# A bidirectional state-space mixer on one core: the logarithm of the step sizes behind the gates, three taps ahead of the states

## The chip, the core and the metric

The kernel runs on one core of a Trainium2 chip. The core has a matrix engine (PE, with its weight loads shown apart as PEld), a vector engine (DVE), an activation engine (ACT), a general-purpose engine (POOL) and a queue processor (SP), which issues most of the transfers here. The engines run their own instruction streams in order and wait for each other by semaphores. The metric is the device time of one execution in microseconds, the median of several runs.

## What is computed

An input of 8 batches x 1024 tokens x 128 channels passes three blocks: attention (L0), a mixer that scans the tokens in both directions (L1_attn), and a filter bank (L1_ffn). The change lies in the mixer and in the last part of the attention, where the mixer's first step sizes are made. For each direction the mixer computes

```python
zxbcdt = x @ in_proj
z, xbc, dt = jnp.split(zxbcdt, [D_INNER, D_INNER + CONV_DIM], axis=-1)
xp = jnp.pad(xbc, ((0, 0), (K - 1, 0), (0, 0)))
conv = sum((xp[:, i:i + l, :] * conv_w[:, i] for i in range(K))) + conv_b
xbc = jax.nn.silu(conv)
xh, Bm, Cm = jnp.split(xbc, [D_INNER, D_INNER + D_STATE], axis=-1)
dt = jax.nn.softplus(dt + dt_bias)
A = -jnp.exp(A_log)
y = _ssd(xh, dt, A, Bm, Cm) + xh * D[None, None, :, None]
yg = y.reshape(b, l, D_INNER) * jax.nn.silu(z)
yn = yg * jax.lax.rsqrt(jnp.mean(yg * yg, -1, keepdims=True) + EPS) * norm_w
return yn @ out_proj
```

K is 4. The second direction does the same on the reversed tokens with other weights. `_ssd` cuts the tokens into chunks of 64: within a chunk a decay-weighted product of C, B and x, between chunks a state that is passed on with a decay. The two parts that the change moves are one tap of `conv` and the logarithm in `softplus`.

## The kernel before

The mixer (from about 450 to 1010 us of the span) handles 16 units, each a batch b and a direction d, in the order (0,0), (0,1), (1,0) and so on. The order of the instructions on every engine is written out by hand (`manual_schedule`): they run in the order in which the Python code issues them. One pass of the loop `for at, u in enumerate(units[:-1])` (line 1285 on) works on three units: it finishes `last`, carries u through its states and outputs, and prepares `following`. Where u is of the first direction and a batch b + 1 is left (b = 0 to 6), the pass also turns that batch's tokens and makes its step sizes for both directions (`fresh`).

What the prediction needs of a pass, in order of issue:

- `going = steps(...)`, a generator, makes the step sizes. Softplus is max(v, 0) + log(1 + exp(-|v|)) with a correction: v and -|v| on DVE (`sp_v`, `sp_e`), the exponential on ACT (line 509), 1 + e on DVE (`sp_u`, line 512), the logarithm on ACT (`sp_l`, line 514), and the rest (`dt`, `da`, lines 516 to 521) on DVE. The code between two `yield`s is issued at one `next(going)`.
- `end(last, ...)` projects `last` (PE, `spo`), and `scale_rows(last)` scales the rows on ACT (eight activations, line 1216). A `next(going)` follows, which holds lines 512 and 514.
- `weigh_decays(u, 1)` and `convolve(following, 0, ...)` on DVE: the convolution of channels 0 to 127 of `following`. The tap with the bias is on ACT (`first_tap`, line 972), the three others are DVE instructions of 128x1024 (line 980). Two of them are issued here.
- `project_z` and `activate_z` for two halves: PE computes `pz`, ACT makes the gates `zs` by Silu (line 993). Then `first_tap(following, 1)`.
- `from_row(following, ...)` on POOL (line 924) starts the decays `lm` of `following`. A dependence added by hand puts it behind `following.convolved`, the last tap issued by then, where u is of the first direction. `between(following, AF.Relu, 1.0)` on ACT (line 934) follows it.
- `chunk_states(u)` on PE (`pst`, line 1082), `pass_states(u)` on DVE (lines 1096 and 1099), with four transfers `moved` out of `state` that SP issues (line 1112), two at the middle and two at the end.
- `next(going)`: lines 516 to 521.
- The third tap, then `activate_x(following, 0)` on ACT (Silu, line 985), `project_bc` on PE (`pb`, 16 matmuls, line 1002), `activate_bc` on ACT (`bt`, `ct`, line 1018), three taps for the other 128 channels, `outputs(u, 0)` on PE (`sy`), `add_decays` (`pdec`, copied out as `cums` and `dsum`), `activate_x(following, 1)`, `outputs(u, 1)`, `add_rows(last)`.
- The next pass begins with `turn_decays` (`cs`), `take_decays` and `turn_x` (`sx` on PE, which reads both `xs`; `xdt` on DVE).

PSUM buffers of the pool `ps_w` are two and taken in turn: `pb` takes the one that the first `pz` had, so it waits for the first gate. `pst` takes those of `spo` and `misc` in the pool `ps_s`.

ACT holds one set of function tables at a time. The exponential, the logarithm and Silu are in three different sets here, and an `ACT_TABLE_LOAD` stands in the stream ahead of each activation whose function the active set lacks.

In the attention, whose loop counts slots n, the step sizes of batch 0 are made at slots 117 (three parts), 121 (lines 512 and 514) and 123 (the rest).

Of the kernel before, what the change touches and what calls it, by code (L numbers as in the profile page):

```python
# [45 lines left out]
def fast_kernel(ctx: ExitStack, tc: tile.TileContext, a: dict, out: bass.AP, bad: bass.AP):  # L46
# [420 lines left out]
    pad = KC - 1  # L467
# [12 lines left out]
    def steps(b, seq, pd):  # L480

        xt = seq["xt"]

        def small(tag):
            return tokens.tile([P, NT, n2], F32, tag=tag, name=f"{tag}{b}")

        def wide(t):  # L490
            return t.rearrange("p d h -> p (d h)").unsqueeze(1).to_broadcast([P, NT, n2])

        pd = pd[:, : NT * n2].rearrange("p (j h) -> p j h", j=NT)
        for j in range(NT):
            nc.tensor.matmul(
                pd[:, j, :],
                lhsT=xt[:, pad + j * P : pad + (j + 1) * P],
                rhs=wdt.rearrange("p d h -> p (d h)"),
                start=True,
                stop=True,  # L500
            )
        yield
        v = small("sp_v")
        nc.vector.tensor_tensor(v, pd, wide(dtb), ALU.add)
        e = small("sp_e")
        nc.vector.tensor_scalar(e, v, -1.0, None, ALU.mult)
        nc.vector.tensor_tensor(e, e, v, ALU.min)
        yield
        nc.scalar.activation(e, e, AF.Exp)
        yield  # L510
        u = small("sp_u")
        nc.vector.tensor_scalar(u, e, 1.0, None, ALU.add)
        lg = small("sp_l")
        nc.scalar.activation(lg, u, AF.Ln)
        yield
        nc.vector.scalar_tensor_tensor(u, u, -1.0, e, ALU.add, ALU.subtract)
        nc.vector.tensor_tensor(lg, lg, u, ALU.subtract)
        dt = small("dt")
        nc.vector.scalar_tensor_tensor(dt, v, 0.0, lg, ALU.max, ALU.add)
        da = tokens.tile([P, 2, NH, NT], F32, tag="da", name=f"da{b}")  # L520
        nc.vector.tensor_tensor(
            da.rearrange("p d h j -> p j d h"),
            dt.rearrange("p j (d h) -> p j d h", d=2),
            nega.unsqueeze(1).to_broadcast([P, NT, 2, NH]),
            ALU.mult,
        )
        seq["dt"], seq["da"] = dt, da
# [63 lines left out]
    with ExitStack() as s:  # L591
# [179 lines left out]
        going, making, coming = transform_taps(p1, ps_t, tables), transforms(p1, tables), qkv(0)  # L771
# [14 lines left out]
        for n in range(len(units) + 2):  # L786
            if n < len(units):
                prs[n] = scores(*units[n])
            if 2 <= n and units[n - 2][2] % 2:
                b, half, j = units[n - 2]  # L790
                total(b, half)
                if j == NT - 1:
                    ending = weighted(b, half, avs[half], sums["d"])
            if 1 <= n < len(units) + 1:
                b, half, j = units[n - 1]
                weigh(b, half, j, prs.pop(n - 1))
                if j == NT - 1:
                    nc.vector.tensor_copy(avs[half], sums["o"])
            if n % 8 in (0, 1, 3, 5, 7):
                next(ending, None)  # L800

            if n % 16 == 14 and n // 16 + 2 < B:
                coming = qkv(n // 16 + 2)
            if n % 16 in (14, 15, 1, 3, 5, 6, 7, 10, 11, 12, 13):
                next(coming, None)
            if n % 16 in (4, 6, 8, 12, 14):
                next(mixing, None)
            if n >= 16 * (B - 1):
                next(going, None)
            if n in (9, 25, 41, 57, 73):  # L810
                next(making, None)

            if n in (99, 115):
                norm = normalize(bridge, n // 112)
            elif n in (103, 119):
                norming = normalized(n // 112, bridge, *norm)
                next(norming)
            elif n in (105, 122):
                next(norming, None)
            elif n == 113:  # L820
                turn_tokens(0, seqs[0], ps_t.tile([P, T], F32, tag="t", name="px0"))
            elif n == 117:
                sizes = steps(0, seqs[0], ps_t.tile([P, T], F32, tag="t", name="pd0"))
                for _ in range(3):
                    next(sizes)
            elif n in (121, 123):
                next(sizes, None)
        assert not [*mixing, *making, *going, *coming]

# [8 lines left out]
    with ExitStack() as s:  # L838
# [46 lines left out]
        def turn_decays(u):  # L885

            nc.tensor.transpose(u.pcs, u.cums[:, 0], ident[: NT * NH, : NT * NH])
            u.cs = p2.tile([P, NH, NT], F32, tag="cs", name=f"cs{u.tag}")
            nc.scalar.copy(u.cs, u.pcs.rearrange("p (h j) -> p h j", h=NH))
# [80 lines left out]
        def first_tap(u, n):  # L970
            xp, body = u.xp[n]
            nc.scalar.activation(
                u.xs[:, n, :], xp[:, body], AF.Identity, bias=cb[u.d][:, n, :], scale=cw[u.d][:, n, pad : pad + 1]
            )

        def convolve(u, n, taps=range(pad)):
            acc, xp = u.xs[:, n, :], u.xp[n][0]
            for i in taps:
                at = i if u.d == 0 else pad - i
                u.convolved = nc.vector.scalar_tensor_tensor(  # L980
                    acc, xp[:, at : at + T], cw[u.d][:, n, i : i + 1], acc, ALU.mult, ALU.add
                )
# [294 lines left out]
        for at, u in enumerate(units[:-1]):  # L1277
            following = units[at + 1]
            after_it = units[at + 2] if at + 2 < len(units) else None

            fresh = u.b + 1 if u.d == 0 and u.b + 1 < B else 0
            turn_decays(following)
            if at == 0:
                between(u, AF.Relu, 1.0)
            take_decays(following)
            between(u, AF.Exp, -1.0, (0,))
            turn_x(u)
            weigh_start(u, u.convolved)
            if last:
                add_x(last)  # L1290
            turn_b(u)
            if fresh:
                turn_tokens(fresh, seqs[fresh], wide_psum(ps_w, f"px{fresh}"))
            between(u, AF.Exp, -1.0, (1,))
            project_x(following, 0)
            copy_x(following, 0)
            if last:
                gate(last, 0)
                gate(last, 1)
            project_x(following, 1)  # L1300
            copy_x(following, 1)
            causal(u)
            decayed_x(u)
            weigh_decays(u, 0)
            going = iter(())
            if fresh:
                going = steps(fresh, seqs[fresh], wide_psum(ps_w, f"pd{fresh}"))
            if last:
                end(last, ps_s, (lambda: next(going)) if fresh else None)
            elif fresh:  # L1310
                next(going)
            next(going, None)
            next(going, None)
            first_tap(following, 0)
            if last:
                scale_rows(last)
            next(going, None)

            b = (u.b + 2) % B
            norm = None  # L1320
            if u.d == 1 or u.b == B - 1:
                norm = normalize(bridge, b)
            weigh_decays(u, 1)
            convolve(following, 0, range(pad - 1))
            for n in range(2):
                project_z(u, n)
                activate_z(u, n)
            first_tap(following, 1)
            for _ in normalized(b, bridge, *norm) if u.d else ():
                pass  # L1330
            from_row(following, shifted[-1] if u.d else following.convolved)
            between(following, AF.Relu, 1.0)
            chunk_states(u)
            pass_states(u)
            next(going, None)
            if stored:
                reload(stored)
            stored = None
            convolve(following, 0, range(pad - 1, pad))
            activate_x(following, 0)  # L1340
            project_bc(following)
            activate_bc(following)
            convolve(following, 1)
            outputs(u, 0)
            if after_it:
                add_decays(after_it)
            activate_x(following, 1)
            outputs(u, 1)
            if last:
                add_rows(last)  # L1350
                stored = last if last.d else None
            last = u

        u = units[-1]
# [1104 lines left out]
```

## Time and profile before

| what | us |
|---|---|
| median of 3 runs (lowest, highest) | 1420.11 (1420.01, 1421.38) |
| the profiled execution | 1414.25 |
| its span | 1412.4 |
| PE busy in the span | 1325.0 |
| DVE busy | 1093.9 |
| ACT busy | 916.0 |
| POOL busy | 530.2 |
| one table load on ACT | 1.28 |
| logarithms, in the whole kernel | 8, of 0.26 each |
| DVE taps (line 980), in the whole kernel | 96, 121.7 in total |

The profile is of one execution, which here was 5.9 us shorter than the median of the runs. A timeline line gives the start, the length, the engine, the line of the kernel, the operation, the tile written and the tiles read, the shapes and how many instructions are merged; in brackets stands how long the engine was idle before, and whom it waited for. `x28` with 5.46 us is 28 instructions that took 5.46 us together. A line of the waits gives the total in us, how often, and the longest. "issue" is idle time for which the profile shows no cause. `PEld` is the weight load of a matmul.

### The profile page before, as it was taken

The page shows a single profiled execution, that of the slowest core. Times are in us where ns is not written, and L with a number is a line of the kernel's source. Part 1 is how long each engine was busy: PE and PEld are TensorE (multiplying, and loading weights), DVE is VectorE, ACT ScalarE, POOL GpSimd, SP SyncE. Part 2 cuts the span into 40 slices and gives each one's busy share as a digit, 9 for nine tenths or more (in the row PEclk, how much of TensorE's full clock was granted, in tenths as well). Part 3 has the DMA queues.
Part 4 walks back from the last instruction along what each step waited for, and adds up shares of the span by engine and source line. Part 5 has one row for each costly group of instructions (what it writes and reads, how often), then busy time and mean ns, then how long its engine had stood idle before and what let it go on. Part 6 is the DMA issues. An engine that isn't in the chain of part 4 may idle for free. (4 is left out here: it accounts for less than half of the span.)

```text
span 1412.4 us, 45313 instructions
## 1 busy us (share of the span) xinstructions
PE 1325.0 (94%) x19798; PEld 836.2 (59%) x19798; DVE 1093.9 (77%) x2141; ACT 916.0 (65%) x1423; POOL 530.2 (38%) x510
## 2 busy tenths in 40 slices
PE   5999999999999899999999999998799899999977
PEld 2323333233333466666666666665689899999964
DVE  6789888787768698978897988889644677777745
ACT  3766666766757777878787878786454555555530
POOL 2426865875610333425243434343476111111100
PEclk9999999999999999999999999999999999999999
DMA  7101111110000543434344445441459233222257
GB/s 179 46 1 31 46 38 38 38 50 27 8 1 2 124 86 77 107 77 106 82 102 91 104 92 114 89 110 42 135 189 233 76 86 81 72 78 71 71 186 299
DMA packets 139382, 123.09 MB, mean 87 GB/s; under 512 B 44808, under 2 KB 118152, under 8 KB 135080
## 3 DMA queue, kind: packets, MB, share of 16 engines
q1 hardware_dynamic: 137048, 115.93, 32.1%
q10 hardware_dynamic: 2128, 4.19, 0.8%
q8 instruction: 157, 2.57, 0.8%
q14 instruction: 49, 0.40, 0.1%
HBM read 78.15 MB, written 34.08 MB: 79 GB/s over the span
## 5 line engine op out<-in xcount | busy, mean ns | idle before, releaser
L707 ACT ACTIVATE pr<-pt 128x1024 f32<-128x1024 f32 x256 | 248.1, 1021 | 114.9 <-PE pt L702 113.5
L732 DVE TENSOR_TENSOR two<-pr,pr 128x1024 f32<-128x1024 f32 x128 | 162.3, 1308 | 19.2 <-ACT pr L707 18.7
L1525 ACT COPY gs<-pg 128x512 f32<-128x512 f32 x256 | 132.4, 603 | 64.1 <-PE pg L1512 48.3
L1523 DVE COPY gs<-pg 128x512 f32<-128x512 f32 x256 | 158.7, 683 | 14.7 <-PE pg L1512 9.7
L702 PE MATMUL pt<-q,k 32*128 32x512 f32 x1024 | 157.6, 648 | 9.4 <-ACT pr L707 4.7
L1512 PE MATMUL pg<-taps,mst 32*128 32x128 f32 x4096 | 145.6, 281 | 4.2 <-ACT gs L1525 3.4
L1512 PEld LDWEIGHTS pg<-taps,mst 32*128 32x128 f32 x4096 | 133.8, 190 | 16.2 <-issue 11.4
L723 PE MATMUL po<-pr,v 128*32 128x512 f32 x1024 | 139.7, 603 | 0.0
L938 POOL TENSOR_TENSOR ec<-ec,ct 128x2048 f32<-128x2048 f32 x16 | 83.6, 5226 | 131.8 <-ACT cums L880 69.8
L1546 PE MATMUL py<-gs,u 128*32 128x128 f32 (+1 forms) x4096 | 128.5, 277 | 1.2 <-issue 1.2
L1002 PE MATMUL pb<-bxt,wbc 128*128 128x512 f32 x256 | 115.7, 605 | 11.0 <-ACT zs L993 11.0
L980 DVE SCALAR_TENSOR_TENSOR xs<-xp,cw,xs 128x1024 f32<-128x1024 f32 x96 | 121.7, 1281 | 1.7
L1546 PEld LDWEIGHTS py<-gs,u 128*32 128x32 f32 (+1 forms) x4096 | 112.4, 141 | 8.7 <-issue 1.5
L1535 POOL TENSOR_SCALAR u<-u 128x512 f32<-128x512 f32 x16 | 23.9, 1495 | 227.8 <-DMA u<-ud 114.0
L702 PEld LDWEIGHTS pt<-q,k 32*128 32x128 f32 x1024 | 46.6, 185 | 87.2 <-issue 33.1
L1002 PEld LDWEIGHTS pb<-bxt,wbc 128*128 128x128 f32 x256 | 47.7, 191 | 69.3 <-issue 54.9
L1099 DVE SCALAR_TENSOR_TENSOR state<-state,dec,pst 128x64 f32<-128x64 f32 x448 | 87.3, 274 | 1.5 <-DVE state L1096 0.5
L1208 POOL TENSOR_TENSOR rms<-rms_v,mhalf 128x8 f32<-128x8 f32 x16 | 27.1, 1696 | 159.7 <-DVE rms_v L1206 159.7
L723 PEld LDWEIGHTS po<-pr,v 128*32 128x32 f32 x1024 | 27.6, 110 | 88.3 <-issue 84.1
L924 POOL TENSOR_TENSOR lm<-cs,lm 128x2048 f32<-128x2048 f32 x16 | 57.9, 3620 | 46.9 <-DVE xs L980 31.4
L743 PE MATMUL pd<-two,ones 128*32 128x512 f32 x512 | 73.9, 612 | 0.2
L1178 PEld LDWEIGHTS spo<-wo,y 128*128 128x128 f32 x512 | 62.2, 192 | 15.3 <-issue 10.2
(288 smaller groups left out, 2757.7 us busy)
## 6 DMA issues: line engine op xcount, KB each, us to landing
lm<-cd SPq DMA_DIRECT2D x32, 512.0 KB
ec<-cd SPq DMA_DIRECT2D x32, 512.0 KB
ud<-sp SPq DMA_DIRECT2D x8, 1024.0 KB
u<-ud SPq DMA_DIRECT2D x32, 256.0 KB
yd<-sums SPq DMA_DIRECT2D x32, 256.0 KB
moved<-state SPq DMA_DIRECT2D x48, 128.0 KB
room<-yd SPq DMA_DIRECT2D x6, 1024.0 KB
X<-in_x SPq DMA_DIRECT2D x8, 512.0 KB
```

The costliest lines, as they stand in the source:

```text
L702: nc.tensor.matmul(pt[:, i, :], lhsT=k[rows, j * P : (j + 1) * P], rhs=q[rows, cols], start=True, stop=True)
L707: nc.scalar.activation(pr[:, 2 * g : 2 * g + 2, :].rearrange("p i t -> p (i t)"), pt.rearrange("p i t -> p (i t)"), AF.Exp, scale=SCALE,)
L723: nc.tensor.matmul(po[rows, :], lhsT=vs[b][:, j, rows], rhs=pr[:, h, :], start=(j == 0), stop=(j == NT - 1))
L732: nc.vector.tensor_tensor(two, sums["pr"][:, 2 * g : 2 * g + 2, :], pr[:, 2 * g : 2 * g + 2, :], ALU.add)
L938: t = nc.gpsimd.tensor_tensor(u.ec, u.ec, u.ct.unsqueeze(1).to_broadcast([P, NH, NT, L]), ALU.mult)
L980: u.convolved = nc.vector.scalar_tensor_tensor(acc, xp[:, at : at + T], cw[u.d][:, n, i : i + 1], acc, ALU.mult, ALU.add)
L1002: nc.tensor.matmul(u.pb[:, i * 512 : (i + 1) * 512], lhsT=wbc[u.d][:, k, :], rhs=xt[:, at : at + 512], start=(k == 0), stop=(k == KC - 1),)
L1099: nc.vector.scalar_tensor_tensor(u.state[:, k, h, :], u.state[:, k - 1, h, :], u.dec[:, c, h, j : j + 1], u.pst[c][:, j, h, :], ALU.mult, ...
L1512: nc.tensor.matmul(pts[g][:, e, :], lhsT=mst[rows, n * 4 + e, :], rhs=taps[rows, cols].rearrange("p f q m i -> p (f q m i)"), start=True, ...
L1523: nc.vector.tensor_copy(to, frm)
L1525: nc.scalar.copy(to, frm)
L1546: nc.tensor.matmul(py[t * 32 : t * 32 + 32 - 16 * m, q // 2, :], lhsT=u[:, i, m:, :, :, q * FC + f].rearrange("p k b i -> p (k b i)"), rhs ...
```

## The change

The logarithm gets a `yield` of its own ahead of it, so that 1 + e and the logarithm are issued at different places. In the mixer 1 + e stays behind `scale_rows`, and the logarithm is issued behind the gates and the first tap of the other channels, ahead of `from_row` and the Relu. In the attention 1 + e moves from slot 121 to slot 120, and the logarithm stays at 121.

In passes whose u is of the first direction (d = 0), all three DVE taps of channels 0 to 127 are issued ahead of the states (`pad - u.d` is 3), where two were. In the other passes (d = 1) it stays at two and one.

```diff
@@ -510,6 +510,7 @@
         yield
         u = small("sp_u")
         nc.vector.tensor_scalar(u, e, 1.0, None, ALU.add)
+        yield
         lg = small("sp_l")
         nc.scalar.activation(lg, u, AF.Ln)
         yield
@@ -823,7 +824,7 @@
                 sizes = steps(0, seqs[0], ps_t.tile([P, T], F32, tag="t", name="pd0"))
                 for _ in range(3):
                     next(sizes)
-            elif n in (121, 123):
+            elif n in (120, 121, 123):
                 next(sizes, None)
         assert not [*mixing, *making, *going, *coming]
 
@@ -1321,11 +1322,13 @@
             if u.d == 1 or u.b == B - 1:
                 norm = normalize(bridge, b)
             weigh_decays(u, 1)
-            convolve(following, 0, range(pad - 1))
+            soon = pad - u.d
+            convolve(following, 0, range(soon))
             for n in range(2):
                 project_z(u, n)
                 activate_z(u, n)
             first_tap(following, 1)
+            next(going, None)
             for _ in normalized(b, bridge, *norm) if u.d else ():
                 pass
             from_row(following, shifted[-1] if u.d else following.convolved)
@@ -1336,7 +1339,7 @@
             if stored:
                 reload(stored)
             stored = None
-            convolve(following, 0, range(pad - 1, pad))
+            convolve(following, 0, range(soon, pad))
             activate_x(following, 0)
             project_bc(following)
             activate_bc(following)
```

In the instruction streams of the changed kernel, the third tap also is the one that `from_row` waits for, and one table load more stands in each of the seven passes: the gates need Silu, the logarithm its own set, and `activate_x` Silu again.

## The prediction

> **What bounds the kernel now.** The page first: PE is busy for 94% of the span, but that is an average over stages. The chain that ended last reaches back only to 1014.58 us, behind the stage that is changed, so for the mixer I read waits and timelines. First the windows by stage and PE's list of waits, both for 480 to 945 us, the seven batches that loop through the mixer:
>
> ```profile
> 480.00:945.00 465.00, 442.58 (x6870) 301.59 (x6869) 395.95 (x867) 370.48 (x589) 172.55 (x95) 1.00 0.42 95
> PE pb L1002 <- ACT zs L993: 10.7, 14, 1.3
> PE sb L1048 <- DVE xdt L1034: 6.2, 14, 0.4
> PE sy L1147 <- issue: 3.5, 5, 0.8
> ```
>
> Columns of the first line: stretch, length, busy PE, PEld, DVE, ACT, POOL, clock, DMA share. PE is busy 442.6 of 465 us; the rest is nearly all in the next three lines (total, times, longest). PE is the bound, and its largest remaining hole is `pb` waiting for the gates `zs`. One pass of the loop in which it is long, u = (1, first direction), on ACT:
>
> ```profile
> 550.83 2.15 ACT L1216 ACTIVATE y<-spo,rms 128x128 f32<-128x128 f32 x8
> 553.00 1.28 ACT L514 ACT_TABLE_LOAD   x1
> 554.29 0.26 ACT L514 ACTIVATE sp_l<-sp_u 128x64 f32<-128x64 f32 x1
> 554.57 1.28 ACT L993 ACT_TABLE_LOAD   x1
> 555.86 1.94 ACT L993 ACTIVATE zs<-pz 128x1024 f32<-128x1024 f32 x2
> 557.69 1.24 ACT L972 ACTIVATE xs<-xp,cb,cw 128x1024 f32<-128x1024 f32 x1
> 558.82 2.00 ACT L934 ACTIVATE lm<-lm 128x1024 f32<-128x1024 f32 x2
> 563.77 1.06 ACT L985 ACTIVATE xs<-xs 128x1024 f32<-128x1024 f32 x1 [2.96 <-DVE xs L980]
> 564.74 1.36 ACT L1018 ACTIVATE bt<-pb,cb 64x512 f32<-64x512 f32 x2
> ```
>
> The logarithm with its table load stands for 1.57 us (555.86 less 554.29) ahead of the gates, and later ACT idles 2.96 us for the third tap. PE, DVE, POOL and the queue in the same pass:
>
> ```profile
> 553.77 1.98 PE L1082 MATMUL pst<-xdd,bg 64*64 64x128 f32 x64
> 556.94 7.13 PE L1002 MATMUL pb<-bxt,wbc 128*128 128x512 f32 x16 [1.20 <-ACT zs L993]
> 569.40 1.97 PE L1031 MATMUL sx<-ident,xs 128*128 128x128 f32 x16
> 551.07 2.60 DVE L980 SCALAR_TENSOR_TENSOR xs<-xp,cw,xs 128x1024 f32<-128x1024 f32 x2
> 555.78 0.29 DVE L1096 COPY state<-pst 128x128 f32<-128x128 f32 x1 [2.11 <-PE pst L1082]
> 556.18 5.46 DVE L1099 SCALAR_TENSOR_TENSOR state<-state,dec,pst 128x64 f32<-128x64 f32 x28
> 562.46 5.12 DVE L980 SCALAR_TENSOR_TENSOR xs<-xp,cw,xs 128x1024 f32<-128x1024 f32 x4
> 553.80 3.62 POOL L924 TENSOR_TENSOR lm<-cs,lm 128x2048 f32<-128x2048 f32 x1 [3.20 <-DVE xs L980]
> 558.59 4.32 SPq L1112 DMA_DIRECT2D moved<-state  x4
> ```
>
> `pst` ends at 555.75, the first gate about 1.03 us after 555.86; `pb`, which takes the PSUM buffer that this gate empties, starts at 556.94. DVE idles 2.11 us for `pst` ahead of the states: room for one tap. From `pb` to `sx` PE runs without a named wait.
>
> **The Trainium skill.** (1) "ScalarE: Activation LUTs", What ACT_TABLE_LOAD costs: 1283 ns for every set, plus some 1380 ns of drain at a switch. The trace agrees on the load (1.28 us) and shows no drain: the load starts 0.02 us after its predecessor's end, and the next activation 0.01 us after the load. (2) Same page, Table sets: `relu`, `copy` and `identity` are in every set. The trace agrees: L934 (Relu) and L972 (Identity) follow the gates with no load. (3) "GPSIMD Engine Reference", Specifications: its SBUF interface is shared with VectorE. In the trace L924 takes 3.62 us each time, and L938 with an operand as large 5.23 us in the mean; so I keep 3.62 for L924, which stays beside the states. (4) "DMA: Bandwidth & Descriptors", Anatomy of one DMA: about 2.0 us fixed (told there for another issuing path). The nearest step in the trace, `yd<-sums`, has 2.39 us.
>
> **The change part by part.** It touches eight passes of the first direction: seven that prepare the next batch's step sizes (b = 0 to 6), and b = 7, which does not and only has its tap moved. Offsets are carried in the pass shown.
>
> *Logarithm behind gates and first tap.* ACT after: `y` ends 552.98; Silu load 553.00 to 554.28; gates from 554.30 (pz's eight matmuls began at 550.23 and end by 553.8, so no wait), 1.56 earlier; first tap 556.13 to 557.37; load 557.4 to 558.7; logarithm to 558.94. In the changed kernel's instruction order a third load stands ahead of `xs`, because Silu is needed again: seven loads more in all, 7 x 1.28 = 9.0 us of ACT, in the idle 2.96. DVE needs the logarithm only behind the states, at 561.5: 2.5 us of room.
> PE: the first gate is read out by 555.35, `pst` ends 555.75, so `pb` starts behind `pst`, about 555.78 for 556.94. The gain is PE's idle time, not ACT's 1.56. In the passes b = 1 to 6 the trace has 1.20, 1.20, 1.19, 1.29, 1.19, 1.19 = 7.26 us there; less 0.03 us each for the change-over, 7.1.
>
> *Third tap ahead of the states.* 1.28 us of DVE (5.12 / 4) moves into the 2.11: taps end 551.07 + 3 x 1.28 = 554.9, before `pst`; states unmoved. POOL's L924 waits for the last tap issued ahead of it, so it starts 1.23 later, 555.03 to 558.65, and Relu, queued behind the logarithm on ACT, may start at 558.94: hidden by 0.3. Relu to 560.94, load to 562.24, `xs` 562.26 for 563.77. `bt` 563.22 (its `pb` ends 555.78 + 7.13 = 562.91), `ct` to 565.97; `cums` waits for `pdec` at 566.05; the second `xs` 566.5 to 567.5, its three taps on DVE ending 562.46 + 3.84 = 566.3. `sx` then begins at 569.40 less 1.16 = 568.24: ACT is there 0.7 us ahead, and PE keeps its gain. Queued behind DVE's taps is add_rows (1.22), done 567.5, before `sx` frees `xdt`.
>
> *Transfers.* The last of the four `moved` transfers is issued by 558.59 + 4.32 = 562.91 both times; with 2.3 us it lands at 565.2; the outputs that read it start behind `pdec` at 566.05 instead of 567.2. Cover left 0.8.
>
> *First pass (b = 0).* There PE idled only 0.20 for the gates and 0.54 us (its loads) for `xs`, with no `y` ahead. Third tap ends 485.72 + 3.86 = 489.58, states 0.2 late; L924 to 493.3; Relu waits for it to 495.35, load, `xs` 496.67 for 497.36. That ends the wait before `sx`: 0.67 gained.
>
> *Last pass (b = 7).* No logarithm. DVE waits only 0.28 us for `pst` (state at 959.28), so the tap puts the states off 1.0 us, and `moved` lands near 966.1 + 1.25 + 2.3 = 969.6, where the second outputs would begin near 968.8. Bounds 0 and 1.0 lost; I take 0.5, since PE's 1.65 us stall there at 971.91 has no named cause and may swallow it or not.
>
> *Step sizes before the mixer (slot 120).* `sp_u`, 0.18 us, moves before a DVE copy that waited 1.25 us for PE; its logarithm starts at its table load's end anyway. Nothing; bounds 0.1 either way.
>
> SP's and POOL's orders are unchanged. What follows (the second direction) hangs on `cs` and `sx`, so it moves as a whole; behind the mixer likewise.
>
> Sum: 7.1 + 0.67 - 0.5 = 7.3 us. The profiled execution took 1414.25 (span 1412.4, 1.85 around it) and goes to 1407.0. The median of the runs shown is 1420.11, 5.9 above it; I take the same absolute gain: 1412.8.
>
> **Rivals.** (a) *Loads dearer, slower.* If the loads at the two new places cost the page's drain too, 2 x 1.38 = 2.76 us, `xs` starts 565.0, `bt` 566.0, `cums` 568.8, second `xs` ends 570.3: 0.9 later than `sx` now. Six passes 5.4, b = 0 some 2.0: 1420.1 + 7.4 = 1427.5. It decides from 1.85 us a pass on (569.40 less 567.55). For: ACT has no idle time left there. Against: no load in the trace shows a drain. (b) *The moved states are late.* If `moved` lands not 2.3 but 3.8 us after its issue, (566.7 for 566.05), the second outputs give back 0.66 of the 1.16 a pass: 6 x 0.5 + 0.67 - 0.5 = 3.2 us left, 1416.9. Against: in second-direction passes the first outputs follow their transfers by some 3.5 us and no DMA wait shows. (c) *Hidden anyway.* The unnamed stalls in `sy` (3.5 us, 5 times) grow as PE's pauses go, or `moved` takes 4.3 us: 1420. For: nothing in the profile says what they are. (d) *It doesn't do what it says:* the logarithm's wait or a gate's wait for `pz` stays first. `pz` is done half a microsecond before; under one in a hundred, counted in (c).
>
> **Numbers.** Forecast 0.74, its own range 1410.8 to 1414.5: high gain 7.26 for PE's six holes + 0.67 + 1.4 of unnamed stalls that fall away, 9.3; low 6 x 1.0 + 0.6 less the 1.0 of b = 7, 5.6. (b) 0.11, (c) 0.06, (a) 0.09. Faster by over 0.2% (2.8 us, about what a measurement tells from no change): 0.74 + 0.11 = 0.85; within 0.06; slower 0.09. The range must hold 0.8: the forecast's with 0.8 us for the runs' own spread below, and up to (b): 1410 to 1417.
>
> **What would show it.** `pb L1002 <- ACT zs` falls from 10.7 to about 3.5 us in the mixer (second direction's 0.46 a pass is left); eight loads at L514 stay and seven more at the line of `xs`; `xs <- DVE xs` falls from 21 us to near 0; `state <- pst` from about 2.1 to 0.8 a pass. I am wrong if loads start with a gap of over 1 us, if `sx` waits for `xs`, or if the outputs wait for `moved`.

## The result, and the profile after

The changed kernel takes 1410.35 us (median of 5 runs, 1410.17 to 1414.42), the kernel before 1420.01 beside it (1419.80 to 1421.38): ratio 0.9939, interval 0.9921 to 0.9956, so 6 to 11 us less. The measured time lies inside the forecast range of 1410 to 1417, only 0.35 us above its lower end, and 0.45 us below the forecast's own range of 1410.8 to 1414.5. The forecast ratio, 0.9949 (1412.8 of 1420.11), lies inside the measured interval. (In the description of the kernel before, the loop over the units was put at line 1285; it begins at line 1277.)

First the same list of waits as before, PE from 480 to 945 us (total, times, longest), of the changed kernel:

```profile
PE sb L1049 <- DVE xdt L1035: 6.2, 14, 0.4
PE sy L1148 <- issue: 3.8, 5, 0.9
PE pb L1003 <- ACT zs L994: 3.2, 7, 0.5
PE pz L948 <- DVE sp_v L504: 0.3, 1, 0.3
```

The wait of `pb` for the gates fell from 10.7 to 3.2 us, 14 times to 7: what is left is the second direction's. The wait of `sx` for `xs` (0.4) is gone. That is 7.9 us in this stretch. Next the pass u = (1, first direction) on ACT, in its timeline:

```profile
552.88 2.15 ACT L1217 ACTIVATE y<-spo,rms 128x128 f32<-128x128 f32 x8
555.05 1.28 ACT L994 ACT_TABLE_LOAD   x1
556.34 1.94 ACT L994 ACTIVATE zs<-pz 128x1024 f32<-128x1024 f32 x2
558.16 1.24 ACT L973 ACTIVATE xs<-xp,cb,cw 128x1024 f32<-128x1024 f32 x1
559.42 1.28 ACT L515 ACT_TABLE_LOAD   x1
560.72 0.26 ACT L515 ACTIVATE sp_l<-sp_u 128x64 f32<-128x64 f32 x1
560.88 1.99 ACT L935 ACTIVATE lm<-lm 128x1024 f32<-128x1024 f32 x2
562.87 1.28 ACT L986 ACT_TABLE_LOAD   x1
564.17 1.06 ACT L986 ACTIVATE xs<-xs 128x1024 f32<-128x1024 f32 x1
...
568.04 0.25 ACT L881 COPY cums<-pdec 32x128 f32<-32x128 f32 x1 [0.15 <-PE pdec L879]
568.20 0.23 ACT L883 COPY dsum<-pdec 128x96 f32<-128x96 f32 x1
568.46 1.06 ACT L986 ACTIVATE xs<-xs 128x1024 f32<-128x1024 f32 x1
570.52 0.18 ACT L890 COPY cs<-pdec 128x32 f32<-128x32 f32 x1 [1.00 <-PE pdec L888]
```

The gates start 1.31 us behind the rows' end (2.88 before). Three loads now, each of 1.28 us and each 0.02 us or less behind its predecessor: no drain. From the rows to `ct` ACT has no hole any more. Of its idle 2.96 us the third load fills 1.28; the rest is gone, since the first `xs` starts 9.14 us behind the rows' end, where it started 10.79 behind it. Later ACT waits 1.00 us for PE ahead of `cs`: ACT is still the earlier one. PE and DVE in the same pass:

```profile
555.81 1.98 PE L1083 MATMUL pst<-xdd,bg 64*64 64x128 f32 x64
557.72 7.14 PE L1003 MATMUL pb<-bxt,wbc 128*128 128x512 f32 x16
570.41 1.97 PE L1032 MATMUL sx<-ident,xs 128*128 128x128 f32 x16
553.12 3.92 DVE L981 SCALAR_TENSOR_TENSOR xs<-xp,cw,xs 128x1024 f32<-128x1024 f32 x3
557.82 0.29 DVE L1097 COPY state<-pst 128x128 f32<-128x128 f32 x1 [0.79 <-PE pst L1083]
```

`pb` begins 1.91 us after `pst` began (3.17 before), without a wait: 1.26 us. `sx` begins 14.60 after it, for 15.63: 1.03 us arrive there. DVE still waits 0.79 us for `pst` with three taps done, so the states are not put off.

The two profiled spans differ by only 4.0 us (1412.4 to 1408.4), less than the medians. They must be split. The first copy of `cums` on ACT, where the mixer's own chain starts, comes at 454.35 before and at 458.36 after: the attention was 4.0 us longer in the second execution. The first experiment takes this up. A measure free of it is the time from the exponential of the step sizes (`sp_e`) in the pass b = 1 to that in b = 6, five batches in mid-mixer. It is in the last column of the table.

| kernel | time, ratio to before (interval) | first `cums` at, us | five batches, us |
|---|---|---|---|
| before (two profiles) | | 454.35, 455.02 | 338.16, 337.73 |
| the change (two profiles) | 0.9939 (0.9921 to 0.9956), 0.9933 (0.9918 to 0.9947) | 458.36, 458.39 | 332.82, 332.32 |
| slot 120 undone | 0.9949 (0.9930 to 0.9968) | 456.77 | 332.80 |
| b = 7 with two taps | 0.9938 (0.9922 to 0.9955) | 458.56 | 332.85 |
| logarithm alone | 0.9973 (0.9963 to 0.9983) | 454.91 | 336.28 |
| taps alone | 1.0003 (0.9994 to 1.0013) | 458.39 | 337.78 |
| one more load | 0.9973 (0.9963 to 0.9983) | 456.47 | 335.50 |
| early Silu (two runs) | 0.9926 (0.9910 to 0.9942), 0.9936 (0.9921 to 0.9950) | 458.75, 458.33 | 331.41, 333.06 |
| early Silu, `turn_b` between | 1.0107 (1.0090 to 1.0123) | 458.68 | 352.65 |

### The profile page after: what moved, and what is told of

The parts are those of the page before. It is cut to its first block, busy times and chain, and to the rows that moved or that the text cites. A ratio compares the mean times of both kernels' runs of the same rounds, so it can differ in the third digit from the quotient of the medians.

```text
span 1408.4 us, 45313 instructions
## 1 busy us (share of the span) xinstructions
PE 1331.0 (95%) x19798; PEld 839.0 (60%) x19798; DVE 1095.8 (78%) x2141; ACT 925.0 (66%) x1430; POOL 528.1 (37%) x510
```

## The experiments

### The kernel before, against itself

No edit.

> The kernel before, run against itself. Between the two profiles so far the mixer is 8.5 us shorter up to the pass b = 7, while the attention, in which nothing changed that could act, is 4.0 us longer; PE's granted clock was lower there. Theory (clock): the 4.0 us are of the execution. A second profile of the kernel before has its pass-to-pass lengths in the mixer within 0.3 us of the first (67.4 to 67.8 us from b = 0 to b = 6), and its attention and its clock differ from the first by as much as the changed kernel's did, 2 to 6 us; its time is between 1414 and 1421. Rival (slot 120 or the code's new place costs the attention 4 us): the second profile's attention agrees with the first within 0.5 us.

Ratio 1.0006 (0.9996 to 1.0015). Four of the five batches agree within 0.3 us, one was 0.83 us shorter. The attention did not vary as expected: it is 0.67 us apart, so this run alone does not decide between the theory and its rival. For slot 120 the column of first `cums` decides: the taps alone, without slot 120, start the mixer at 458.39; the logarithm alone, with slot 120, at 454.91. PE's granted clock from 245 to 280 us was 0.95 in the profile of the kernel before and of the logarithm alone, and 0.91 in that of the change and of the taps alone:

```profile
245.00:280.00 35.00, 32.02 (x214) 10.38 (x214) 27.68 (x27) 25.28 (x29) 28.57 (x26) 0.95 0.13 39
```

```profile
245.00:280.00 35.00, 32.02 (x202) 9.12 (x202) 26.96 (x27) 25.35 (x30) 25.96 (x23) 0.91 0.13 39
```

The first line is of the kernel before, the second of the taps alone, both from the windows by stage (the clock is the third number from the end). Neither of these two has slot 120, and up to 489 us their engines run the same instructions in the same order. So the 4 us come neither from slot 120 nor from any other instruction that the change moves. The clock explains less than half of them: compared copy by copy of ACT's exponentials in the attention (`pr`), the taps alone are some 2.2 us late at 37 us of the span already, and only some 1.6 us are added in this window, between 272 and 277 us. That the rest belongs to the single execution is likely but not shown: two profiles of one kernel are never more than 0.67 us apart in this column. The 60 runs of the kernel before that stand beside these experiments lay between 1415.65 and 1424.73: the profiled 1414.25 was lower than any of them.

### The logarithm alone

```diff
-            soon = pad - u.d
+            soon = pad - 1
```

> Only the logarithm (and slot 120) moves; the third tap stays behind the states. Theory (both parts are needed): pb follows pst at once as in the full change, but the first xs still waits for the tap until where it was, and the second xs ends about 569.0 in the scale of the pass shown, so sx gains only some 0.5 of the 1.1 us a pass: 2 to 4 us less than before, ACT xs <- DVE xs still about 20 us in the mixer. Rival (the logarithm is the whole gain, the tap is beside the point): the time of the full change within 1 us.

The ratio is 0.9973: 3.8 us less, and 0.33 us a batch in the five batches against 1.05 for the full change (337.95 in the mean before, less 332.7 in the mean of the four profiles in rows two to four of the table, where both parts stand in full, over five). The wait for the tap was expected at about 20 us and is 11.9, because the logarithm and its load now stand in it. The mechanism is seen in ACT's timeline of the pass b = 1:

```profile
560.52 1.28 ACT L986 ACT_TABLE_LOAD   x1
563.46 1.06 ACT L986 ACTIVATE xs<-xs 128x1024 f32<-128x1024 f32 x1 [1.66 <-DVE xs L981]
...
567.62 1.06 ACT L986 ACTIVATE xs<-xs 128x1024 f32<-128x1024 f32 x1
568.58 0.17 ACT L890 COPY cs<-pdec 128x32 f32<-128x32 f32 x1
```

`cs` follows `xs` with no wait for PE: ACT, held by the tap, is now the later one, and PE's waits for it read

```profile
PE pb L1003 <- ACT zs L994: 3.2, 7, 0.5
PE sx L1032 <- ACT xs L986: 2.1, 5, 0.6
```

PE wins 7.5 us at `pb`, and loses 2.1 again at `sx` for ACT and 1.2 in longer stalls of `sy` (4.7 for 3.5). The rival, that the tap is beside the point, falls.

### The taps alone

```diff
-            convolve(following, 0, range(pad - 1))
+            soon = pad - u.d
+            convolve(following, 0, range(soon))
...
-            convolve(following, 0, range(pad - 1, pad))
+            convolve(following, 0, range(soon, pad))
```

(the rest as before the change)

> Only the third tap moves; the logarithm and its load stay ahead of the gates, no load is added. Theory: pb starts where it did, with PE waiting 1.2 us for zs in each pass b = 1 to 6, so these gain nothing; b = 0 gains 0.5 to 0.7 us of the wait of sx for xs: 0 to 1.5 us less than before, though ACT xs <- DVE xs falls from 21 us to near 0. Rival (ACT's wait for the tap was the bound): 3 us or more less.

The ratio is 1.0003, and the five batches are the old ones. Waits of PE, then of ACT:

```profile
PE pb L1002 <- ACT zs L993: 10.7, 14, 1.3
```

```profile
ACT bt L1018 <- PE pb L1002: 14.4, 7, 2.4
```

ACT's 21 us of waiting for the tap are gone, and 14.4 us of waiting for `pb` have come: the engine is idle at another place. Even the 0.5 us of b = 0 can't be seen in the time. Neither part does the work by itself, 3.8 and 0 us; together they bring about 8.7 (0.9939 of 1420).

### Slot 120 undone

```diff
-            elif n in (120, 121, 123):
-                next(sizes, None)
+            elif n in (121, 123):
+                for _ in range(2 if n == 121 else 1):
+                    next(sizes, None)
```

> The full change, but in the attention 1 + e and the logarithm are both back at slot 121. Theory: the same as the full change, within 0.5 us; the logarithm starts at the end of its table load either way. Rival (slot 120 costs the attention): 2 to 4 us less than the full change.

The ratio is 0.9949 with an interval that holds the full change's 0.9939, and the five batches take 332.80 us. The rival asked for a time 2 to 4 us below the full change, and this run is not below it.

### The pass b = 7 with two taps

```diff
-            soon = pad - u.d
+            soon = pad if fresh else pad - 1
```

> The full change, but the pass b = 7, which makes no step sizes, keeps two taps ahead of the states and one behind. The prediction took this pass to lose 0.5 us (0 to 1.0). Theory as predicted: this kernel is 0 to 1 us faster than the full change, the states of that pass start 0.3 us after the second tap again. Rival, from the profile of the changed kernel, where sx of that pass starts 0.6 us earlier after pst than before: the tap gains there too (ACT is earlier), and this kernel is 0.5 to 1.5 us slower than the full change.

The ratio is 0.9938 (0.9922 to 0.9955): no difference that the times can show; half a microsecond is too little for them. The rival's 0.5 to 1.5 us are not seen, and of the theory's 0 to 1 us the 0 comes out. The traces say it more sharply. The tap does what the prediction said to the states: they start 2.96 us after `pst` began, and 2.01 without it. But `sx` begins 14.52 us after `pst` with the tap and 14.59 without it. Take away the one stall without a named cause that `sy` has in this pass (1.03 and 1.09 us), and 13.5 us are left in both; so too in the second profile of the changed kernel (15.05 with a stall of 1.54) and in the kernel before (15.15 with 1.65). Only the stall varies. The outputs do not wait for the states. SP's line of that pass in the changed kernel:

```profile
958.50 4.32 SPq L1113 DMA_DIRECT2D moved<-state  x4
```

The third transfer is issued by 962.15, the last by 962.82. The first matmul that waits for the third one's semaphore starts at 964.10, the first that waits for the last one's at 964.68, and neither has a gap ahead of it. So they had landed at most 1.95 and 1.87 us after the end of their issue.

### One more load

```diff
+                nc.scalar.activation(spare, mhalf, AF.Exp)
```

(behind the Relu, in the seven passes that make step sizes)

> The full change, and in the seven passes an added exponential of one column right behind the Relu, whose result is not used: one table load (1.28 us) and some 0.2 us more on ACT between the logarithm and the first xs. Theory (PE bounds, ACT is 0.9 us ahead of sx in the changed kernel's profile): 0.5 to 0.7 us a pass beyond that room, up to 1.5 in b = 0: 4 to 6 us slower than the full change, and sx or cs then waits for ACT. Rival (ACT has nothing to spare): 1.5 x 7 = 10 us slower. Rival (the table loads are hidden anyway): within 1 us.

The ratio is 0.9973, so 4.8 us of the gain are lost, as expected; in the five batches it is 0.56 us a batch. ACT's timeline (b = 1) shows the load and what it holds up:

```profile
562.62 1.28 ACT L1338 ACT_TABLE_LOAD   x1
563.91 0.20 ACT L1338 ACTIVATE spare<-mhalf 128x1 f32<-128x1 f32 x1
564.12 1.28 ACT L986 ACT_TABLE_LOAD   x1
...
569.57 1.06 ACT L986 ACTIVATE xs<-xs 128x1024 f32<-128x1024 f32 x1
570.53 0.17 ACT L890 COPY cs<-pdec 128x32 f32<-128x32 f32 x1
```

In PE's list of waits `sx` now stands with

```profile
PE sx L1032 <- ACT xs L986: 2.0, 6, 0.6
```

Of the 1.5 us that were added about 0.6 show in the time: ACT's room in the changed kernel is some 0.9 us a pass. A fourth load fits only in part.

### The second direction's load ahead of the rows

```diff
             first_tap(following, 0)
+            if u.d:
+                nc.scalar.activation(spare, mhalf, AF.Silu)
             if last:
                 scale_rows(last)
```

> The full change, and in passes of the second direction a Silu of one column, whose result is not used, right ahead of the scaled rows: the table load that stood between rows and gates moves into ACT's wait of 1.8 us for rms. No load is added. Theory: pb of these passes then follows pst at once, and the 0.46 us that PE waits there for zs go, seven times: 3 us less than the full change, pb <- zs in the mixer from 3.2 to near 0. Rival (the next thing is as late: pst, whose buffer the rows empty, or the load not fitting the wait): within 1 us of the full change.

The ratio is 0.9926 beside 0.9938 for the kernel with two taps in b = 7. Since the intervals overlap, this kernel and the changed one ran once more, beside each other:

> The changed kernel once more, beside the next two on the same chip. Theory: 0.994 of the kernel before within 0.002, and PE's waits without a named cause in sy differ from the first profile's (3.8 us in the mixer) by a microsecond or more, since the same kernel shows them at 0.3 to 1.9 us apiece in other profiles. Rival (they belong to the change): the same stalls at the same lengths.

> The table load of the second direction's gates ahead of the scaled rows, once more, beside the changed kernel. Theory: 7 x 0.46 = 3 us less than the changed kernel of this call, of which the unnamed stalls may take one or two back: 1 to 3 us. Rival: no difference, within 1 us.

The ratios are 0.9936 and 0.9933: no difference that can be measured. The intervals reach some 2 us to each side, so a gain of 1 us could hide in them. PE's waits say more, first of the changed kernel's second profile, then with the early load:

```profile
PE sb L1049 <- DVE xdt L1035: 6.2, 14, 0.4
PE sy L1148 <- issue: 4.2, 7, 1.0
PE pb L1003 <- ACT zs L994: 3.2, 7, 0.5
```

```profile
PE sy L1148 <- issue: 7.2, 9, 1.4
PE sb L1049 <- DVE xdt L1035: 6.2, 14, 0.4
```

The 3.2 us of `pb` are gone, and the stalls in `sy` that have no named cause are 3.0 us longer (6.3 us in the other run of this kernel). They stand at the same places: the outputs of the second direction's passes near 602, 670, 868 and 935 us stall 0.78, 0.74, 0.89 and 0.84 in the changed kernel's first profile, and 1.21, 1.16, 1.35 and 1.30 in this one of the early load, 0.42 to 0.46 more at each (0.15 to 1.02 more in the other). What PE gained at `pb` it waits some 11 us later. As to the changed kernel's two profiles, `sy` differs by 0.4 us, less than expected (with 0.6 more at `sx`): the stalls belong to places in the stream, and only their lengths vary.

No run was made for what PE waits for there, but the traces show what comes ahead of each stall. The page of every profile here lists a queue whose transfers are of the kind `instruction`; the entries are transfers, MB and share:

```profile
q8 instruction: 157, 2.57, 0.8%
```

That is 16 KB each, one in about 8.6 us of the mixer. In the mixers of the twelve profiles, 69 times two matmuls of the same outputs start more than 0.6 us apart. All 69 times the second one starts 2.2 to 3.0 us after such a transfer began. The stall near 602 us, first in the changed kernel, then with the early load (second profile):

```profile
601.83 0.27 PE L1148 MATMUL sy<-ec,state 64*64 64x64 f32 x2 [0.78 <-issue]
602.28 0.27 PE L1148 MATMUL sy<-ec,state 64*64 64x64 f32 x2 [1.21 <-issue]
```

The transfers ahead of them begin at 599.56 and 599.88. Counted from the start of `pst` in the same pass that is 12.31 and 12.10 us. With the early load PE reaches the place 0.50 us earlier (13.08 for 13.58), but the transfer comes hardly earlier, and the stall ends at 14.51 for 14.58. At the other three places too the transfer begins 12.0 to 12.9 us after `pst` with the early load and 12.1 to 12.6 without it. So it looks as if PE waits there for its next instructions, at a time that its own progress at `pb` does not move. This rests on coinciding times in the traces; no run moved these transfers by themselves.

### turn_b between the halves of turn_x

```diff
-            turn_x(u)
+            turn_x(u, (0,))
+            turn_b(u)
+            turn_x(u, (1,))
             weigh_start(u, u.convolved)
...
-            turn_b(u)
```

(on top of the early load; `turn_x` takes the halves to issue)

> As the one before, and turn_b stands on PE between the two halves of turn_x, so that the half's PSUM buffer is emptied by DVE while PE works on the other one. Theory (PE is the bound, and sb <- xdt, 0.44 us in each of 15 passes, is the largest named wait left): that wait goes, 4 to 6 us less than the kernel without it, unless DVE, whose second xdt now comes 1 us later, is late at the next place. Rival (DVE then sets the pass): no gain or slower.

The ratio is 1.0107: 15 us slower than the kernel before, and 24 slower than the early load alone. The rival was right: the wait of `sb` for `xdt` is gone from PE's list, but this order costs more than that wait. DVE's timeline at the start of a pass, and the wait that then leads PE's list:

```profile
574.93 1.22 DVE L1036 TENSOR_TENSOR xdt<-sx,dt 128x1024 f32<-128x1024 f32 x1 [2.01 <-PE sx L1033]
578.51 1.22 DVE L1036 TENSOR_TENSOR xdt<-sx,dt 128x1024 f32<-128x1024 f32 x1 [2.36 <-PE sx L1033]
579.65 2.71 DVE L1163 SCALAR_TENSOR_TENSOR y<-xs,dcol,sy 128x512 f32<-128x512 f32 x4
582.28 2.35 DVE L1174 TENSOR_TENSOR y<-y,zs 128x1024 f32<-128x1024 f32 x2
```

```profile
PE spo L1180 <- DVE y L1174: 16.8, 20, 1.3
```

DVE idles 2.36 us between its two `xdt`, all that is queued behind the second one is late, and `spo` waits for the gated `y` 16.8 us in place of the 6.2.

## Why the prediction was right

*The bound and the place.* Right. The hole in PE ahead of `pb` was the thing to win, and PE's idle time, not ACT's 1.56 us, set the gain. `pb` was to follow `pst` with 0.03 us of change-over; it follows with none.

*The size of a pass.* 1.16 us were forecast, 1.05 measured over five batches. 1.26 us are won at `pb`, and 1.03 arrive at `sx` in the pass shown: some 0.2 us are lost inside the outputs, in a stall at 568.7 that no named wait explains, and here too an `instruction` transfer began 2.4 us earlier.

*ACT's sum.* Right to 0.3 us: the forecast had the first `xs` start 9.28 us after the rows' end, measured 9.14; it had ACT ahead of PE by 0.7 us, and measured are 1.0 by ACT's wait at `cs` and 0.9 by the added load. The drain that the Trainium skill ("ScalarE: Activation LUTs", What ACT_TABLE_LOAD costs) adds to a load shows at none of the three loads, which ends the rival that was slower.

*The third tap.* That it moves into DVE's wait without putting off the states is right. Its own worth was not stated as a term: the sum gave the logarithm 7.1 us with the tap's cost hidden. The runs show how much hangs on it: the logarithm without the tap brings 3.8 us of the 8.7, and in the five batches 1.7 of 5.2.

*The pass b = 7.* The step that failed. The term was a loss of 0.5 us, with bounds of 0 and 1.0, and in the traces it is 0. The states are 0.95 us late as forecast, but the landing was taken at 2.3 us after the issue, from the step of another, larger transfer, and is at most 1.9. The last transfer also is needed 0.6 us later than was assumed, since the second outputs begin with matmuls that read only the third.

*The stalls without a name.* They didn't grow with the change beyond 0.3 to 0.7 us (3.5 to 3.8 and 4.2), so the rival of a gain that is hidden anyway did not come true here. It did with the early Silu, which the prediction's reasoning would have put at 3 us. The prediction found nothing in the profile that says what these stalls are; the queue of instructions in the same page is a strong hint.

*The sum.* With 6 x 1.05 for b = 1 to 6, 0.62 in b = 0 (0.26 of it at `pb`, the rest where `sx` waited) and no loss in b = 7, the parts give 6.9, where 7.3 was forecast and the times give 8.7 with an interval of 6.2 to 11.2. The mixer as a whole, from the first `cums` to the last projection, takes 554.97 us in the two profiles of the kernel before and 546.4 in the mean of four with the gain in full: 8.6 less. Up to the start of `pst` in b = 7 it is 7.2 less, close to the parts. The other 1.3 to 1.4 come behind it, where nothing but the 0.5 of b = 7 was forecast and where profiles of one kernel differ by 1.3 and 2.1 us: scatter, as far as these profiles tell. So the mechanism is right and so is its size; that the time came out inside the range with 0.35 us to spare owes something to scatter, for the runs of one kernel spread over 9 us.

## What to carry to other kernels

Where two engines reach a meeting point within a microsecond of each other, moving work out of the way of one of them pays only as far as the other follows: here the logarithm alone gave 3.8 us, the taps alone nothing, both 8.7. Put an added cost into a hole that is known, and measure the room left by filling it with one more of the same. The largest named wait of the bounding engine is no promise: here 6 us seemed to be had and 24 were lost; before reordering for it, follow what is queued behind the consumer that would have to move. For a stall without a named cause, see whether transfers of the kind `instruction` begin ahead of it.

## What the runs showed of the hardware that was not expected

Three table loads in a row on ACT, with work between them, cost 1.28 us each and no more than 0.02 us around them. Of the transfers from `state` to `moved`, one of 128 KB and one of 96 KB had landed 1.95 and 1.87 us or less after the end of their issue. PE stalls 0.2 to 1.9 us at fixed places of a long stream of 64x64 matmuls. The profile names no releaser for them, but each of the 69 long ones ends 2.2 to 3.0 us after a 16 KB transfer of the kind `instruction` began. In both profiles of the early load they took back, nearly one for one, what PE had won some 11 us earlier.
